# Where the image statistics of a sample are taken: from the local to the global attention's turns, and two group norms on ScalarE

## The chip, the core and the metric

The kernel runs on one core of a Trainium2 chip. The metric is the time of one execution on the device, in microseconds (us). A core has TensorE (PE in the profile; its weight loads are PEld), VectorE (DVE), ScalarE (ACT), GpSimd (POOL) and SyncE (SP), which here only issues transfers. Each engine works through its own list of instructions in order, and waits where an instruction needs the result of another engine.

## What is computed

Four layers follow one another on four samples of 56 x 56 x 128 values. Each takes a group norm of its input and adds its result to it:

```python
x = x + _L0_conv_ref(_gn(x), ...)   # window attention, global attention, MLP
x = x + _L1_conv_ref(_gn(x), ...)   # edge layer
x = x + _L2_conv_ref(_gn(x), ...)   # spectral attention over the channels' images
x = x + _L3_conv_ref(_gn(x), ...)   # convolution
```

Layer 2 normalizes every image (one channel of one sample, 56 x 56) by its own mean and variance, of the values that its group norm gives. These are the image statistics of which this document speaks.

## The kernel before, in words

The samples are taken one after the other through layers 0 and 1 (`first_layers`, called for b = 0 to 3), with the channels in the 128 partitions. For each sample:

1. **Local attention** (`fast_windows`, L307). The 3136 tokens lie in 8 groups of 392. A loop over n sets the order by hand: in step n group n+2 is normed (`norm`, L366, through the helper at L193, on DVE), group n is projected (`project`, L371 to L379: TensorE, then the heads' queries w_qd by turns on DVE, L225, and ScalarE, L223), group n-1 is scored, and so on for the later stages. Norms 0, 1 and 2 stand ahead of project(0) on DVE. Three sets of buffers w_xg, w_kT, w_qd, w_vd, w_pT are set to zero by POOL at the start (L339 to L345), w_qd fourth. The order of TensorE, ScalarE and DVE is the order of the program; POOL's memsets are placed by the scheduler.
2. **Global attention** (`fast_layer`, L615). The queries lie in 7 blocks of 448 and the keys in 24 chunks of 128, for four heads. One unit is one head's scores of one chunk. A turn (L840) makes 7 units: `scores(0)` of four units into PSUM banks 0 to 3, `scores(1)` of three into banks 4 to 6 (L818), one exponential for each (L821) into a ring of 28 slots (7 chunks), then some `values` matmuls (L684). The first 28 units are made beside the rest of the local attention's projections; the turns after that are counted here from 1, and there are 92. A bank holds 512 values for each partition, a score uses 448. The softmax's denominators need the sum over the chunks: DVE adds the chunks (`f_acc`, L669 and L673), 5 of the 24 are added by transfers (`f_far`: the first on SP, L661, four on POOL, L663), and DVE adds f_far last but one (L672). After a block `finish` takes f_acc through TensorE (L715 to L721), and DVE inverts the result (L728). The remainder of the keys is scored at L704, and from block 3 on an earlier block is centred at L743. At the end a square root's table is loaded (L862).
3. MLP, then the **edge layer** (`e_` tiles), whose result x1 goes to memory (x2d, L2812).

**The image statistics** of sample b-1 are taken beside sample b's layer 0. `normed_images` (L1480) is a generator: each `yield` ends a step. Its steps are 28 pairs of `bn_stats` on the 56 rows of x1 (L1492), their aggregate (L1496), a small matmul (L1499) that averages over the channels of a group, three small operations, a second small matmul (L1508), the copy of its result s_var and six small operations, a square root on ScalarE (L1523), four operations for mean and scale, a third matmul (L1532, s_mean) and its copy to `norm`, a fourth (L1541, s_sq) and its copy to s_d, four instructions that norm x1 in place (L193 on x), after the last of them two transfers on SP (xat L1548, xad L1550), and a last root (L1552) with two operations. `yield "root"` stands ahead of each of the two roots.

In the kernel before, `fast_windows` takes one such step after every stage of the local attention (`run` and `step`), a matmul's result goes into a bank of the rotation that the stages use (`bank`), and the two roots are put right behind the local attention's own roots (`root`, L445), for which the table is loaded anyhow. Sample 0 has no sample ahead of it, so there are no steps in its local attention. The last sample's statistics are taken later, in layer 2, and are not concerned.

Of the kernel before, what the change touches and what calls it, by code (L numbers as in the profile page):

```python
# [12 lines left out]
F32 = mybir.dt.float32  # L13
AF = mybir.ActivationFunctionType
ALU = mybir.AluOpType
# [4 lines left out]
P = 128  # L20
B = 4
HH = 56
TOK = HH * HH
NB = 448
# [167 lines left out]
def apply_norm(k, out, xt, mr):  # L192
    k.nc.vector.tensor_scalar(out, xt, mr[:, 0:1], mr[:, 1:2], ALU.subtract, ALU.mult)  # L193
# [110 lines left out]
    mlp(k, w, xf, xw, x1, st)  # L304


def fast_windows(k, w, xw, xf, mr, beside, Q, K, V, h1, inverse):  # L307

# [6 lines left out]
    nc, tc = k.nc, k.tc  # L317
# [3 lines left out]
    N = 8 * WIN  # L321
# [4 lines left out]
    with ExitStack() as es:  # L326
# [6 lines left out]
        for i in range(BUFS):  # L333
            xg = big.tile([P, N + 16], F32, name="w_xg%d" % i)
            kT = big.tile([P, N + 16], F32, name="w_kT%d" % i)
            qd = big.tile([P, 8, 4, WIN], F32, name="w_qd%d" % i)
            vd = big.tile([P, 4, 4, 2, 33], F32, name="w_vd%d" % i)
            pT = big.tile([P, 16 * WIN + 16], F32, name="w_pT%d" % i)
            nc.gpsimd.memset(xg[:, N:], 0.0)  # L339
            nc.gpsimd.memset(kT[:, N:], 0.0)  # L340
            nc.gpsimd.memset(pT[:, 16 * WIN:], 1.0)
            nc.gpsimd.memset(qd, 0.0)
            nc.gpsimd.memset(vd, 0.0)
            for par in range(2):
                nc.gpsimd.memset(vd[halves[par], :, :, par, 32], 1.0)  # L345
            fixed.append((xg, kT, qd, vd, pT))
# [16 lines left out]
            return slice(g * N, (g + 1) * N)  # L363

        def norm(g):
            apply_norm(k, fixed[g % BUFS][0][:, :N], xw[:, g * N:(g + 1) * N], mr)  # L366

        def project(g):
            xg, kT, qd, vd, pT = fixed[g % BUFS]
# [73 lines left out]

        def root(i):
            nc.scalar.activation(inverse[:, i, :], roots[i][:, :N], AF.Sqrt, scale=1024.0, bias=eps)  # L445
            step(True)

        def invert(i):
            nc.vector.reciprocal(inverse[:, i, :], inverse[:, i, :])
# [25 lines left out]
                nc.vector.tensor_copy(V[:, chunk:chunk + m, :].rearrange("p a c -> p (a c)"), pm[:, :m * P])  # L475
                chunk += m

        steps = beside(bank)
        root_next = False

        def step(root):
            nonlocal root_next
            if root or not root_next:
                root_next = next(steps, None) == "root"

        def run(*stages):
            for stage, g in stages:
                if 0 <= g < NG:
                    stage(g)
                    step(False)  # L490

        norm(0)
        norm(1)
        for n in range(NG + 1):
            run((norm, n + 2), (project, n), (score, n - 1), (value, n - 2), (turn, n - 3), (output, n - 4),
                (central, n - 5), (variance, n - 6))
        variance(3)
        root(0)
# [2 lines left out]
        invert(0)  # L501
        run((turn, 7), (output, 6), (central, 5), (output, 7), (central, 6), (variance, 4), (variance, 5))
        run((divide, 0), (central, 7), (attended, 0), (variance, 6), (divide, 1), (variance, 7))
        while not root_next and next(steps, "end") not in ("root", "end"):
            pass
        root(1)
        nc.scalar.activation(eps, k.eps, AF.Exp)
        run((attended, 1))
        invert(1)
        for _ in steps:  # L510
            pass
    rest = [((divide, 2),)] + [((attended, g), (divide, g + 1)) for g in range(2, 7)] + [((attended, 7),)]

    def finish(n):
# [97 lines left out]
LAST_ONES = (22, 23)  # L612


def fast_layer(k, w, xw, xf, x1, st, beside, mr):  # L615

# [6 lines left out]
    with ExitStack() as es:  # L625
# [3 lines left out]
        va = big.tile([P, 25, P], F32, name="f_va")  # L629
        oT = big.tile([P, TOK], F32, name="f_oT")  # L630
        inverse = big.tile([P, 2, 8 * WIN], F32, name="f_inverse")
        use = fast_windows(k, w, xw, xf, mr, beside, qT, kT, va, oT, inverse)

        ring = es.enter_context(tc.tile_pool(name="f_ring", bufs=1)).tile([P, RING, NB], F32, name="f_ring")
        wk = es.enter_context(tc.tile_pool(name="f_wk", bufs=2))
# [111 lines left out]
        def deviation(i0, m, n):  # L747
            for q in range(m):
                nc.tensor.matmul(pm[32 * q:32 * q + 32, n, :NB], k.ones_c[:, 0:32], qT[:, blk(i0 + q)],
                                 start=True, stop=True)  # L750
            r = kT[:32 * m, blk(i0)]
            nc.scalar.activation(r, pm[:32 * m, n, :NB], AF.Sqrt, scale=1024.0, bias=eps[:32 * m])
            nc.vector.reciprocal(r, r)
# [54 lines left out]
        with tc.manual_schedule(engines={mybir.EngineType.PE, mybir.EngineType.Activation, mybir.EngineType.DVE}):  # L808
            t, special, n_bank = 0, 0, 0

            def scores(n):
                nonlocal t
                m = (4, 3)[n]
                ss = bank(n)
                for i in range(m):
                    j, c = divmod((t + i) // 4, 24)
                    h = (t + i) % 4
                    nc.tensor.matmul(ss[:, i, :NB], kT[heads[h], c * P:(c + 1) * P], qT[heads[h], blk(j)],  # L818
                                     start=True, stop=True)
                slot = t % RING  # L820
                nc.scalar.activation(ring[:, slot:slot + m, :], ss[:, :m, :NB], AF.Exp, scale=scale)  # L821
                for q in range(t // 4, (t + m) // 4):
                    queue.append((*divmod(q, 24), WHOLE))
                    add(*divmod(q, 24))
                t += m

            def other_banks():
                nonlocal n_bank
                n_bank += 1
                return pm[:, 4 + n_bank % 3, :]  # L830

            windows_rest, n_rest = use(other_banks)
            for n in range(n_rest):
                scores(0)
                values(2)
                windows_rest(n)
                ready.extend(queue)
                queue.clear()
            turn = 0
            while t < 96 * NBLK:  # L840
                scores(0)
                scores(1)
                values(ROOM[turn % 4] + (len(ready) > 3))
                turn += 1
                ready.extend(queue)
                queue.clear()
                if special < NBLK and t >= 96 * special + 7 and (not special or hasattr(blocks[special - 1], "raw")):
                    j = special
                    special += 1
                    remainder(j)  # L850
                    if j >= 3:
                        centre(j - 3, 6)
                    if not j:
                        ready.append((0, 24, WHOLE))
                    else:
                        started = hasattr(blocks[j], "po")
                        finish(j - 1, j if started else None)
                        if not started:
                            ready.append((j, 24, WHOLE))

            last = NBLK - 1
            nc.scalar.activation(root, k.eps, AF.Sqrt)  # L862
            deviation(0, 4, 3)
            while ready:
                values(4)
            copied = finish(last)
            divide(0, 4, 4)
            copied()
            centre(4, 2)
            hidden(0)  # L870
            hidden(1)
            result(0)
            nc.tensor.matmul(pm[:, 5, :NB], w.wo, oT[:, blk(last)], start=True, stop=True)
            output(last, pm[:, 5, :NB])
            centre(5, 6)
            hidden(2)
            centre(6, 7)
            result(1)
            deviation(4, 3, 5)
            hidden(3)  # L880
            result(2)
            divide(4, 3, 5)
            for wi in range(3, 8):
                if wi < 7:
                    hidden(wi + 1)
                result(wi)
            statistics(7)
# [592 lines left out]
def normed_images(k, w, st, b, wk, bank, xp, xad, xat):  # L1480
# [48 lines left out]
    yield  # L1529
    nc.vector.tensor_scalar(sq, sq, mr[:, 1:2], mr[:, 1:2], ALU.mult, ALU.mult)  # L1530
    ps = bank()
    nc.tensor.matmul(ps[:, 64:64 + HH], k.ones_c, mean, start=True, stop=True)  # L1532
    yield
    nc.vector.tensor_copy(st.norm[:, b, 0, :], ps[:, 64:64 + HH])
    nc.vector.tensor_sub(d, mean, st.norm[:, b, 0, :])
    yield
    nc.vector.tensor_mul(d, d, d)
    nc.vector.scalar_tensor_tensor(sq, d, float(HH), sq, ALU.mult, ALU.add)
    yield
    ps = bank()  # L1540
    nc.tensor.matmul(ps[:, 128:128 + HH], k.ones_px, sq, start=True, stop=True)  # L1541
    yield
    nc.vector.tensor_copy(d, ps[:, 128:128 + HH])
    yield
    for t in range(0, HH, 14):
        apply_norm(k, x[:, t:t + 14, :], x[:, t:t + 14, :], mr)
# [1205 lines left out]
def build(k, packs, I, out):  # L2752
# [3 lines left out]
    with ExitStack() as es:  # L2756
# [16 lines left out]
        with tc.tile_pool(name="w01", bufs=1) as wp, tc.tile_pool(name="io", bufs=1) as io:  # L2773
            xw = io.tile([P, TOK], F32, name="xw")
            with ExitStack() as pre:
# [24 lines left out]

                input_norms(k, x, wp, wk, psum, between())
                small_scores = scores_are_small(k, bounds, wp, wk)

            def first_layers(front, x, to, loaded=False):
                if not loaded:
                    nc.sync.dma_start(xw, x)
                xf = io.tile([P, TOK], F32, name="xf")
                st = io.tile([P, 9, 6], F32, name="x1_st")
                front(k, w0, xw, xf, x1, st)
                edge_layer(k, w1, x1, st)  # L2810
                if to is not None:
                    nc.sync.dma_start(to, x1)  # L2812
# [6 lines left out]

            with tc.If(small_scores > 0) as small:  # L2820
                for b in range(B):
                    first_layers(lambda *a: fast_layer(*a, functools.partial(norms, b - 1), k.mr[:, b, :]), I["x"][b],
                                 x2d[b] if b < B - 1 else None, loaded=b == 0)
            with small.Else():
                with tc.For_i(0, B, 1) as b:
# [78 lines left out]
```

## Time and profile before

| | us |
|---|---|
| median of 3 runs (lowest, highest) | 3538.7 (3538.6, 3540.94) |
| the profiled execution | 3539.16 |
| its span, from first to last instruction | 3537.4 |
| TensorE busy in the span | 3314.4 (94%) |
| DVE, ScalarE, POOL busy | 2706.5, 2101.2, 1252.5 |
| local attention of samples 0, 1, 2, 3: from ScalarE's first w_qd to the first exponential of the global attention | 67.6, 79.5, 79.4, 78.7 |
| global attention of samples 0 and 1: from there to the root after it (L862) | 365.0, 365.0 |

The profile is one execution. Its page shows each engine's busy time, the chain of instructions that ended last (75% of it on TensorE, 15% on DVE) and the costliest groups of instructions. A timeline lists instructions of one stretch: start, duration, engine, line, operation, output and inputs, how many were merged (x2; the duration is then that of the stretch), and in brackets the idle time of the engine before it with what ended it. A matmul in float32 is recorded as two. The table "by windows" gives each engine's busy time in a stretch, its number of instructions in brackets, the clock that TensorE was granted (1.00 is full) and what the transfers moved.

### The profile page before, as it was taken

How to read it: one execution, taken by the hardware profiler on the slowest of the kernel's cores; microseconds unless marked ns; L12 is line 12 of the kernel's file. 1: busy time of each engine (PE TensorE's matmuls, PEld its weight loads, DVE VectorE, ACT ScalarE, POOL GpSimd, SP SyncE). 2: the span in 40 equal slices, each digit the busy share in tenths (PEclk: the TensorE clock that was granted, in tenths of full speed). 3: DMA queues.
4: the chain of work that ended last, by engine and by line, in shares of the span. 5: the costliest groups of instructions: out<-in, count | busy, mean ns of one | idle time of the engine just before them, and what ended most of it. 6: DMA issues, size and time to landing. Idle time of an engine off the chain costs nothing.

```text
span 3537.4 us, 64240 instructions
## 1 busy us (share of the span) xinstructions
PE 3314.4 (94%) x27710; PEld 1425.1 (40%) x27710; DVE 2706.5 (77%) x2566; ACT 2101.2 (59%) x2199; POOL 1252.5 (35%) x764
## 2 busy tenths in 40 slices
PE   6999998889999898999999889999888899999998
PEld 4433333353333434333343443333337443336664
DVE  6588868867888597688859858887795778886776
ACT  4688866558888564788857558887553012214442
POOL 1000007600000491000019400000673778884686
PEclk8999999999999999999999999999998999999999
DMA  2143420014343000444310024442003037753101
GB/s 104 43 93 86 96 52 19 19 48 95 87 92 84 19 1 20 100 95 95 89 45 1 19 61 95 92 98 60 37 14 99 6 70 175 183 139 92 55 19 55
DMA packets 98011, 243.40 MB, mean 69 GB/s; under 512 B 64456, under 2 KB 69832, under 8 KB 92712
## 3 DMA queue, kind: packets, MB, share of 16 engines
q0 software_dynamic: 16128, 102.77, 14.4%
q1 hardware_dynamic: 74872, 123.61, 12.0%
q10 hardware_dynamic: 6720, 12.85, 1.3%
q8 instruction: 219, 3.59, 0.4%
q14 instruction: 72, 0.59, 0.1%
HBM read 79.43 MB, written 31.33 MB: 31 GB/s over the span
## 4 chain that ended last, share of the span: by engine, by line
PE 75%; DVE 15%; ACT 4%; issue 3%; POOL 2%; DMA 0%; DVEq 0%; POOLq 0%; ACTq 0%
PE f_pm L818 18%; PE f_pm L684 15%; PE u_po L1941 8%; DVE e_td L1222 7%; PE e_acc L1277 3%; PE q_acc L1795 3%; PE f_pm L791 2%; PE f_pm L770 2%; PE e_pa L1190 2%; ACT f_ring L821 1%; PE f_pm L464 1%; PE o_d L2204 1%; DVE f_acc L673 1%; PE o_d L2601 1%; PE f_pm L715 1%
## 5 line engine op out<-in xcount | busy, mean ns | idle before, releaser
L821 ACT ACTIVATE f_ring<-f_pm 128x1792 f32<-128x1792 f32 (+1 forms) x764 | 1093.8, 1482 | 229.3 <-PE f_pm L818 181.6
L673 DVE TENSOR_TENSOR f_acc<-f_acc,f_ring 128x1792 f32<-128x1792 f32 x468 | 947.6, 2025 | 191.3 <-ACT f_ring L821 160.2
L818 PE MATMUL f_pm<-f_qT,f_kT 32*128 32x448 f32 x5376 | 725.4, 571 | 15.7 <-ACT f_ring L821 5.1
L684 PE MATMUL f_pm<-f_ring,f_va 128*32 128x448 f32 (+1 forms) x6304 | 589.8, 490 | 0.0
L663 POOL DMA_DIRECT2D f_far<-f_ring x112 | 96.6, 862 | 1333.3 <-ACT f_ring L821 1062.6
L1222 DVE TENSOR_TENSOR e_td<-e_a,e_pc 128x1792 f32<-128x1792 f32 (+1 forms) x288 | 493.1, 1778 | 15.1 <-ACT e_c L1210 15.0
L1224 POOL TENSOR_TENSOR e_tp<-e_a,e_c 128x1792 f32<-128x1792 f32 (+1 forms) x152 | 453.6, 3021 | 74.4 <-issue 42.5
L818 PEld LDWEIGHTS f_pm<-f_qT,f_kT 32*128 32x128 f32 x5376 | 260.0, 183 | 418.0 <-ACT f_ring L821 304.6
L684 PEld LDWEIGHTS f_pm<-f_ring,f_va 128*32 128x32 f32 x6304 | 163.8, 109 | 410.1 <-issue 397.8
L1936 DVE TENSOR_TENSOR u_ud<-u_px,u_d 112x1792 f32<-112x1792 f32 x144 | 263.5, 1863 | 39.6 <-PE u_po L1941 35.4
L1277 PE MATMUL e_acc<-e_td,t_edge 128*32 128x448 f32 x2016 | 225.4, 543 | 42.5 <-DVE e_td L1222 42.3
L1226 ACT ACTIVATE e_tp<-e_tp 128x1792 f32<-128x1792 f32 (+1 forms) x152 | 236.9, 1583 | 44.9 <-POOL e_tp L1224 44.4
L1938 POOL TENSOR_TENSOR u_up<-xh,u_d 112x1792 f32<-112x1792 f32 (+1 forms) x72 | 240.8, 3372 | 55.1 <-PE u_po L1941 41.3
L1941 PE MATMUL u_po<-u_ud,AT 112*64 112x448 f32 x1056 | 213.7, 544 | 1.9 <-DVE u_ud L1936 1.9
L1277 PE MATMUL e_acc<-e_tp,t_edge 128*32 128x448 f32 x1120 | 131.1, 540 | 3.3 <-ACT e_tp L1226 3.3
L1277 PEld LDWEIGHTS e_acc<-e_td,t_edge 128*32 128x32 f32 x2016 | 55.5, 109 | 191.1 <-DVE e_td L1222 116.0
L1941 PEld LDWEIGHTS u_po<-u_ud,AT 112*64 112x64 f32 x1056 | 74.3, 138 | 128.8 <-issue 112.9
L728 DVE RECIPROCAL f_den<-f_den 128x448 f32<-128x448 f32 x28 | 82.6, 2951 | 44.9 <-ACT f_den L725 44.9
L1780 POOL TENSOR_TENSOR q_u<-iS,q_g 128x1792 f32<-128x1792 f32 x32 | 102.8, 3235 | 23.0 <-PE q_acc L1795 23.0
L1795 PE MATMUL q_acc<-q_u,S 64*64 64x448 f32 x1024 | 104.6, 553 | 4.4 <-DVE q_u L1782 3.3
L1941 PE MATMUL u_po<-u_up,AT 112*64 112x448 f32 x480 | 103.9, 546 | 2.4 <-POOL u_up L1938 2.4
L1190 PE MATMUL e_pa<-e_xg,t_edge 128*128 128x448 f32 x224 | 101.0, 577 | 5.1 <-DVE e_xg L193 5.1
(526 smaller groups left out, 4435.6 us busy)
## 6 DMA issues: line engine op xcount, KB each, us to landing
f_far<-f_ring POOLq DMA_DIRECT2D x112, 896.0 KB, 6.3
u_d<-dd SPq DMA_DIRECT2D x46, 784.0 KB
f_far<-f_ring SPq DMA_DIRECT2D x28, 896.0 KB
xw<-in_x SPq DMA_DIRECT2D x4, 1568.0 KB
x2d<-x SPq DMA_DIRECT2D x4, 1568.0 KB
xat<-x SPq DMA_DIRECT2D x4, 1568.0 KB
x_xs<-xat ACTq DMA_DIRECT2D x32, 196.0 KB
xm<-x_ev ACTq DMA_DIRECT2D x64, 98.0 KB
```

What stands on the lines that cost most here:

```text
L673: nc.vector.tensor_add(e.acc, e.acc, slots(j, c))
L684: nc.tensor.matmul(e.po[heads[h], part], va[o, c, heads[h]], p, start=(c == 0), stop=(c == 23 and part.stop == NB))
L818: nc.tensor.matmul(ss[:, i, :NB], kT[heads[h], c * P:(c + 1) * P], qT[heads[h], blk(j)], start=True, stop=True)
L821: nc.scalar.activation(ring[:, slot:slot + m, :], ss[:, :m, :NB], AF.Exp, scale=scale)
L1222: nc.vector.tensor_tensor(t, am, cm, ALU.max)
L1224: nc.gpsimd.tensor_sub(t, am, cm)
L1226: nc.scalar.activation(tf, tf, AF.Relu)
L1277: nc.tensor.matmul(acc[quarters[r0 + r], :NB], w.S[:, 0, :], t[:, r].rearrange("p l n -> p (l n)"), start=(g == 0), stop=False)
L1795: nc.tensor.matmul(acc[bp][i][halves[hb % 2], hb // 2, :NB], x[o], u[o, 8 * hb:8 * hb + 8, :].rearrange("p h t -> p (h t)"), start=first, ...
L1936: nc.vector.tensor_mul(u, bc(px[:, :, :NB], 2, m), dm)
L1938: nc.gpsimd.tensor_mul(u, bc(x, 2, m), dm)
L1941: nc.tensor.matmul(po[64 * b2:64 * b2 + 64, :NB], st.AT[:, 8 * i + h0 + q, 2 * bp + b2, :], u[:, b2, q, :], start=(left == 16), stop=(left ...
```

## The change

- `normed_images` is no longer handed to `fast_windows`. `fast_layer` makes the generator (`steps`) and takes one step at the end of each turn of the global attention, from the third turn on, until the second `"root"`; what is left (the last root and two operations) is issued behind the turns, after the table for the square root is loaded. The first root now falls into the turns, between exponentials, so that the built program loads ScalarE's table twice there.
- The results of its four small matmuls go into the 64 values of bank 3 that the scores leave unused (`pm[:, 3, NB:]`).
- Norms 0 and 1 of the local attention are done by ScalarE, as x times scale plus a shift, which is made once for all samples. Norms 2 and on stay on DVE; in step 0 project(0) goes ahead of norm(2). In the built order DVE has norm 2 and norm 3 one after the other, behind project(0) and ahead of project(1).
- POOL's memset of w_qd comes second, not fourth.
- In the built order the local attention of samples 1 to 3 has, from project(0) on, the instructions of sample 0.

```diff
         def norm(g):
-            apply_norm(k, fixed[g % BUFS][0][:, :N], xw[:, g * N:(g + 1) * N], mr)
+            out, x = fixed[g % BUFS][0][:, :N], xw[:, g * N:(g + 1) * N]
+            if g < 2:
+                nc.scalar.activation(out, x, AF.Identity, bias=shift, scale=mr[:, 1:2])
+            else:
+                apply_norm(k, out, x, mr)
...
         def root(i):
             nc.scalar.activation(inverse[:, i, :], roots[i][:, :N], AF.Sqrt, scale=1024.0, bias=eps)
-            step(True)
...
-        steps = beside(bank)
-        root_next = False
-
-        def step(root):
-            nonlocal root_next
-            if root or not root_next:
-                root_next = next(steps, None) == "root"
-
         def run(*stages):
             for stage, g in stages:
                 if 0 <= g < NG:
                     stage(g)
-                    step(False)
...
         for n in range(NG + 1):
-            run((norm, n + 2), (project, n), (score, n - 1), (value, n - 2), (turn, n - 3), (output, n - 4),
+            begin = [(norm, n + 2), (project, n)]
+            run(*(begin if n else begin[::-1]), (score, n - 1), (value, n - 2), (turn, n - 3), (output, n - 4),
                 (central, n - 5), (variance, n - 6))
...
+            steps, rooted = beside(lambda: pm[:, 3, NB:]), 0
             windows_rest, n_rest = use(other_banks)
...
                 scores(1)
                 values(ROOM[turn % 4] + (len(ready) > 3))
                 turn += 1
+                if turn > 2 and rooted < 2:
+                    rooted += next(steps, None) == "root"
                 ready.extend(queue)
...
             nc.scalar.activation(root, k.eps, AF.Sqrt)
+            for _ in steps:
+                pass
             deviation(0, 4, 3)
...
-    nc.tensor.matmul(ps[:, 64:64 + HH], k.ones_c, mean, start=True, stop=True)
+    nc.tensor.matmul(ps[:, 2:2 + HH], k.ones_c, mean, start=True, stop=True)
...
+                k.shift = wp.tile([P, B], F32, name="shift0")
+                nc.vector.scalar_tensor_tensor(k.shift, k.mr[:, :, 0], -1.0, k.mr[:, :, 1], ALU.mult, ALU.mult)
```

## The prediction

> **What bounds the kernel now.** I first read the windows of the sample parts. Sample 0's local attention has no image statistics beside it, sample 1's has. The windows run from ScalarE's first w_qd to the first exponential of the global attention; the third is sample 0's global attention.
>
> ```profile
> core 0: us, PE busy (x) PEld busy (x) DVE busy (x) ACT busy (x) POOL busy (x), PEclk, DMA share, GB/s
> 55.30:122.86 67.56, 65.69 (x650) 43.05 (x646) 38.80 (x80) 43.62 (x76) 3.86 (x12) 0.98 0.01 1
> 695.40:774.86 79.46, 70.48 (x659) 44.14 (x658) 51.37 (x157) 44.16 (x77) 1.95 (x8) 0.95 0.18 41
> 122.86:487.88 365.02, 360.38 (x3242) 123.00 (x3244) 294.90 (x161) 298.98 (x232) 24.26 (x28) 1.00 0.40 89
> ```
>
> See two things. The statistics cost the local attention 79.46 - 67.56 = 11.9 us, although DVE is only 65% busy. The global attention is bound by TensorE: 360.4 of 365.0 us. There DVE (295) and ScalarE (299) have room on average, but each microsecond for which TensorE itself waits is lost.
>
> The timeline of sample 1 (start, duration, then the idle before it) shows how the statistics cost it:
>
> ```profile
> 754.42 0.82 PE L427 MATMUL w_mm<-w_oT,t_first 128*128 128x392 f32 x2
> 758.55 0.67 PE L1541 MATMUL w_late<-s_sq,c_ones_px 128*128 128x56 f32 x2 [3.30 <-DVE s_sq L1538]
> 759.01 1.63 PE L432 MATMUL w_mm<-xf,c_centre 128*128 128x392 f32 x2
> ```
>
> A matmul of 56 columns stood in TensorE's order until DVE, behind a 2.60 us reciprocal (L449), had its input; everything behind it waited 3.30 us, and then ran at half speed (window 760 to 765: clock 0.52). So the small chain hurts by waits in TensorE's order, not by its 20 us of DVE work.
>
> The start of sample 1's local attention:
>
> ```profile
> 689.16 3.70 DVE L193 TENSOR_SCALAR w_xg<-xw,mr 128x392 f32<-128x392 f32 x1
> ...
> 688.77 1.41 POOL L342 MEMSET w_qd<- 128x1568 f32 x1
> ...
> 695.40 0.58 ACT L223 ACTIVATE w_qd<-w_mm,t_first 32x392 f32<-32x392 f32 x1 [10.53 <-DVE w_qd L225]
> ```
>
> The first norm takes 3.70 us beside POOL's memsets, where the median of this row is 0.47.
>
> **Pages.** The Trainium skill, "SBUF — State Buffer", section "SBUF: two separate sides", says that a GpSimd instruction and a two-port Vector instruction lock each other out of a shared port pair for whole instructions, and that ScalarE's ports wait for nobody. The 3.70 against 0.47 us agrees; for the moved norms I go by L223's 0.58. "TensorE: Matmul & The Clock Gate", section "What's actually happening", has the clock halve after about one idle window of 3.4 us. The trace had it after 3.30 us idle in all three samples, but not after the waits of 1.33 us in the edge layer (clock 1.00); I go by the trace and take 3 us as the doubtful edge.
>
> **The change, part by part** (per sample 1 to 3 unless said).
>
> (a) Statistics leave the local attention. Its duration becomes sample 0's, which has exactly that order: 79.46, 79.40 and 78.73 become 67.56. Gain 11.9 + 11.8 + 11.2 = **34.9**.
>
> (b) Norms 0 and 1 on ScalarE, w_qd's memset first. ScalarE idled 10.53 us there. Norm at 688.65 + 0.6, two projections of 0.8, and DVE's first w_qd at 690.3 instead of 694.69; the memset (1.41 us from 688.67) is done at 690.1. But norms 2 and 3 stay on DVE, now ahead of project(1), and POOL's memsets run until 697.4: each waits for the end of a memset, about 694.4 and 696.2. Project(1)'s w_qd then comes at 696.3 instead of 698.97: **2.7**; bounds 1.0 (one memset more) and 4.3 (no lock). For sample 0, 0.5 by the same count. Sum 8.6. One shift of 0.15 us on DVE: nothing, beside the branch.
>
> (c) 28 pairs of statistics (0.33 us each) in the turns of the global attention, one a turn. A turn lasts 3.35 us; DVE's adds are 2.03 (pitch 2.1). At the ends of blocks 0 and 1 DVE finished f_acc at 844.93 and 893.83, TensorE took it at 846.41 and 895.35: 1.5 us in hand; three or four pairs fall behind the last idle, 1.0 to 1.3 us. Cost 0. Block 2's end lies behind the stall of (g): 0. At block 3's end four x norms (0.62) meet 1.7 us in hand: 0.3.
>
> (d) Four small matmuls in TensorE's order: 0.3 each, as 753.00 to 753.26: 1.2.
>
> (e) Their waits. The changed build's order shows each at the end of a turn, right after a turn whose DVE step makes its input. Beside the s_mv matmul (turn 32, TensorE ready at 919.7), DVE still has two adds to 919.9 and then the aggregate of 1.67: wait 2.0. For s_mean (turn 41, ready 954.5), DVE has the reciprocal of f_den and two adds to 956.2, then three small ones: 2.3. For s_t and s_sq three turns of adds lie between: 0. Sum 4.3.
>
> (f) The new banks' release. The small matmul's result stands in the unused columns of bank 3, and the changed order shows that two turns after each small matmul the fourth score matmul of the turn, the one that writes bank 3, waits for DVE: for the copy of that result. The copy is queued behind the adds of its own turn, which need that turn's exponentials. Here is such a turn:
>
> ```profile
> 929.26 1.78 PE L818 MATMUL f_pm<-f_qT,f_kT 32*128 32x448 f32 x14
> ...
> 930.36 2.85 ACT L821 ACTIVATE f_ring<-f_pm 128x1792 f32<-128x1792 f32 x2 [0.51 <-PE f_pm L818]
> ...
> 930.97 1.71 PE L684 MATMUL f_pm<-f_ring,f_va 128*32 128x448 f32 x16
> 932.61 1.78 PE L818 MATMUL f_pm<-f_qT,f_kT 32*128 32x448 f32 x14
> ...
> 928.71 10.54 DVE L673 TENSOR_TENSOR f_acc<-f_acc,f_ring 128x1792 f32<-128x1792 f32 x5 [1.22 <-ACT f_ring L821]
> ```
>
> From a turn's start: exponentials end at 2.7 and 3.95, an add takes 2.1, and TensorE wants bank 3 at 3.35 + 0.75 = 4.1. Counted with each turn's chunks: copy of s_mr behind one add on the first exponential, 4.95 + delay of the aggregate: wait 1.25. Copy of s_var behind three adds, the last on the second exponential: 7.0, wait 3.0. Copy of norm behind two adds: 7.5, wait 3.4. Copy of s_d behind an add delayed by the two before it: 5.9, wait 1.85. Sum **9.5**. Behind TensorE wait ScalarE's exponentials, and POOL's far adds behind those. No row shows this wait; bounds 0 (if DVE were always in time) and 13 (each behind two late adds).
>
> (g) Square root of the variance in turn 38: two table loads and a root on ScalarE. Row L862 gives 1.28 a load and its neighbours touch it; root 0.28: 2.84, of which 0.4 was idle. TensorE's next use of those banks (L704, L743) comes **2.15** later. The last root (0.33) and DVE's 0.7 at the end come before f_kT, which is needed 1.4 us after it is made: 0.
>
> (h) The idles of (f), about 2.7 and 3.1 us, touch the clock's edge; half speed cost 1.5 to 3 us in the local attention. I take 1.
>
> (i) SP: xat and xad leave the gap between stages (762 to 775) and go ahead of block 4's first f_far. Their issue holds SP 7.7 us and they move 3.2 MB in 13 us. A ring slot comes round in 15 us and its transfer needs 7.2. I take 0; at worst 5 us, when the transfers share the time.
>
> **Sum.** Gains 34.9 + 8.6 = 43.5. Costs per sample 0.3 + 1.2 + 4.3 + 9.5 + 2.15 + 1 = 18.45, times 3 = 55.4. Net +11.9. The profiled run took 3539.2 us (span 3537.4 and 1.8 around it), 0.5 above the median of 3538.7, which is within the runs' spread. 3539.2 + 11.9 = **3551**.
>
> **Rivals.**
> *Faster: bank 3 comes free in time.* One mechanism: if the copies are taken before TensorE returns to bank 3, (f) and with it (h) fall: 3539.2 - 43.5 + 3 x 7.95 = 3519.6. For it: DVE waits for ScalarE at most adds (160 us over 161), so it is often on time. Against it: the copy stands behind adds on its own turn's exponentials, and 4.8 is later than 4.1 even without delay. It decides when the four waits sum to under 6.5 us a sample.
> *About the same.* The waits overlap with ScalarE's lag and come to 5 to 8 us: 3533 to 3545.
> *The clock gate and the transfers.* Both long idles halve the clock (2 x 2.3 in place of 1) and xat makes ScalarE wait 2 us for ring slots: +3 x 5.6: 3568.
> *The norms gain nothing* because DVE waits for POOL's last memset: 8.6 down to 3: 3557; inside the first case.
>
> **Numbers.** First case (3545 to 3561) 0.5, gate and transfers 0.18, about the same 0.17, faster 0.15. Likeliest 3551; its own range is 3545 to 3561. Differences under 0.2% (7 us) can't be told from none here: slower 0.68, same 0.17, faster 0.15. Range 3527 to 3567: it cuts off most of the faster case and the worst of the slow one.
>
> **What would show it.** (a) first w_qd to first exponential in samples 1 to 3 near 67.6. (b) DVE's norms 2 and 3 long, project(1)'s w_qd some 7.6 us after POOL's first memset. (e), (f) TensorE idle before the s_mv and s_mean matmuls and before four L818 rows a sample, released by DVE. (g) two loads of 1.28 beside a TensorE idle of 2. (h) a clock under 1 near turns 36 and 43. The global attention at about 382 us in samples 1 to 3, 365 in sample 0. It is wrong if those attentions stay under 379.

## The result and the profile after

The change makes the kernel slower by 0.65%: 3563.9 us (3557.7 to 3564.9, six runs) against 3540.3 (3538.6 to 3542.0, six runs); ratio 1.0065, 95% interval 1.0053 to 1.0078. The forecast was 3551, 3527 to 3567, slower with 0.68. The direction and the range held; the time is 13 us above the likeliest value, and above that case's own range by 3.

The page of the kernel after, first its span, then its first part (busy time), then TensorE's row of score matmuls; the fourth line is that row in the kernel before:

```profile
span 3563.1 us, 64248 instructions
...
PE 3330.2 (93%) x27710; PEld 1432.2 (40%) x27710; DVE 2687.9 (75%) x2559; ACT 2114.9 (59%) x2213; POOL 1252.2 (35%) x764
...
L809 PE MATMUL f_pm<-f_qT,f_kT 32*128 32x448 f32 x5376 | 734.2, 576 | 34.5 <-DVE s_var L1507 8.0
...
L818 PE MATMUL f_pm<-f_qT,f_kT 32*128 32x448 f32 x5376 | 725.4, 571 | 15.7 <-ACT f_ring L821 5.1
```

The span grew by 25.7 us. TensorE has the same number of instructions; it is busy 16 us longer and idle 10 us longer. Ahead of the score matmuls it is idle 34.5 us instead of 15.7, and the largest part, 8.0, was ended by VectorE's s_var, a result of the moved statistics. The windows tell where, in this order: the local attention of sample 1, and the global attention of samples 0 and 1.

```profile
core 0: us, PE busy (x) PEld busy (x) DVE busy (x) ACT busy (x) POOL busy (x), PEclk, DMA share, GB/s
694.86:763.29 68.43, 64.27 (x650) 42.17 (x648) 40.42 (x81) 43.75 (x75) 6.17 (x19) 1.00 0.05 19
124.83:491.50 366.67, 362.03 (x3242) 123.62 (x3244) 294.89 (x161) 299.04 (x231) 24.28 (x28) 1.00 0.40 89
763.29:1152.64 389.35, 372.12 (x3250) 126.23 (x3252) 306.73 (x240) 301.71 (x234) 24.12 (x28) 0.97 0.41 92
```

The local attention gained what was forecast (79.46 became 68.43, at full clock). The global attention of sample 1 paid more: 389.35 us, not 382, with 10 us more of busy TensorE than in sample 0, at a mean clock of 0.97. Its matmuls are the same ones plus four small ones, so most of that busy time is matmuls at half speed.

The timeline of TensorE in sample 1, only the rows that waited over a microsecond in the two blocks (of seven) in which the small matmuls fall; the same two blocks of the kernel before have no such row:

```profile
911.70 0.35 PE L1495 MATMUL f_pm<-s_mv,t_shared 128*128 128x1 f32 x2 [1.64 <-DVE s_mv L1492]
...
927.23 1.88 PE L809 MATMUL f_pm<-f_qT,f_kT 32*128 32x448 f32 x8 [2.64 <-DVE s_var L1507]
...
944.33 0.98 PE L695 MATMUL f_pm<-f_qT,f_kT 32*64 32x448 f32 x8 [1.90 <-ACT f_ring L812]
...
959.19 0.40 PE L1528 MATMUL f_pm<-s_mean,c_ones_c 128*128 128x56 f32 x2 [2.24 <-DVE s_mean L1524]
...
966.65 1.13 PE L809 MATMUL f_pm<-f_qT,f_kT 32*128 32x448 f32 x8 [1.49 <-DVE norm L1530]
...
980.18 1.03 PE L809 MATMUL f_pm<-f_qT,f_kT 32*128 32x448 f32 x8 [1.61 <-DVE s_d L1539]
```

All forecast waits are there but the one for s_mr: L1495 and L1528 are (e), L809 released by VectorE is (f), L695 behind the table loads is (g). Each is shorter than forecast. The windows show what was missed. They are laid on a grid of 3.41 us; read TensorE's busy time in one row and the clock in the next:

```profile
909.43:912.84 3.41, 1.77 (x19) 0.81 (x13) 3.41 (x3) 1.16 (x1) 0.86 (x1) 1.00 0.18 36
912.84:916.26 3.42, 3.42 (x22) 0.94 (x19) 2.04 (x2) 2.85 (x2) 0.00 (x0) 0.50 1.00 201
916.26:919.67 3.41, 3.38 (x38) 1.25 (x30) 1.02 (x4) 1.60 (x2) 0.00 (x0) 1.00 0.18 36
923.08:926.49 3.41, 1.51 (x14) 0.31 (x6) 3.31 (x2) 1.02 (x1) 0.00 (x0) 1.00 1.00 202
926.49:929.90 3.41, 2.67 (x16) 0.83 (x20) 0.85 (x3) 0.72 (x1) 0.00 (x0) 0.50 0.17 34
929.90:933.32 3.42, 3.42 (x24) 1.03 (x19) 2.34 (x2) 2.13 (x2) 0.00 (x0) 0.50 0.00 0
940.15:943.56 3.41, 2.29 (x22) 0.42 (x16) 1.83 (x1) 3.37 (x4) 0.00 (x0) 1.00 0.02 5
943.56:946.97 3.41, 2.44 (x18) 0.66 (x18) 1.48 (x1) 3.41 (x5) 0.00 (x0) 1.00 0.49 202
```

A window with 1.64 us idle is followed by one at exactly half clock, 3.41 us long. The wait of 1.90 us ahead of L695 straddles two windows (1.12 and 0.97 idle), and the clock stays full. So short waits, which the prediction took for harmless below 3 us, can slow the matmuls behind them: 5, 5 and 3 such windows in these two blocks of samples 1, 2 and 3, where the kernel before had none.

**Where the 25.7 us are.** The profiled execution is cut at GpSimd's first memset of a sample, at the first exponential of the global attention, at the reciprocals of f_den that close each block, and at the next sample's memset. From memset to first exponential: 46.2 us gained over four samples. From there to the first reciprocal: 4.8 lost. From the first to the seventh: 22.0, 21.6 and 20.1 lost in samples 1 to 3 and none in sample 0. The rest of the samples: 0.7 lost. Ahead of sample 0: 2.7 lost. Sum 25.7.

### The profile page after: what moved, and what is told of

Read it like the earlier page. It is cut to its first block, busy times and chain, and to the rows that moved or that the text cites. A ratio compares the mean times of both kernels' runs of the same rounds, so it can differ in the third digit from the quotient of the medians.

```text
span 3563.1 us, 64248 instructions
## 1 busy us (share of the span) xinstructions
PE 3330.2 (93%) x27710; PEld 1432.2 (40%) x27710; DVE 2687.9 (75%) x2559; ACT 2114.9 (59%) x2213; POOL 1252.2 (35%) x764
## 3 DMA queue, kind: packets, MB, share of 16 engines
q1 hardware_dynamic: 74872, 123.61, 11.9%
## 4 chain that ended last, share of the span: by engine, by line
PE 74%; DVE 15%; ACT 5%; issue 4%; POOL 2%; DMA 0%; DVEq 0%; POOLq 0%; ACTq 0%
PE f_pm L809 16%; PE f_pm L675 14%; PE u_po L1937 8%; DVE e_td L1218 6%; PE e_acc L1273 3%; DVE f_acc L664 3%; PE q_acc L1791 3%; ACT f_ring L812 3%; PE e_pa L1186 2%; PE f_pm L782 2%; PE f_pm L761 2%; PE w_ss L394 1%; PE f_pm L467 1%; PE o_d L2200 1%; PE f_pm L706 1%
## 5 line engine op out<-in xcount | busy, mean ns | idle before, releaser
L809 PE MATMUL f_pm<-f_qT,f_kT 32*128 32x448 f32 x5376 | 734.2, 576 | 34.5 <-DVE s_var L1507 8.0
L675 PE MATMUL f_pm<-f_ring,f_va 128*32 128x448 f32 (+1 forms) x6304 | 601.8, 499 | 0.0
L809 PEld LDWEIGHTS f_pm<-f_qT,f_kT 32*128 32x128 f32 x5376 | 261.9, 184 | 436.9 <-ACT f_ring L812 295.3
```

What stands on the lines that cost most here:

```text
L675: nc.tensor.matmul(e.po[heads[h], part], va[o, c, heads[h]], p, start=(c == 0), stop=(c == 23 and part.stop == NB))
```

## The experiments

Each run is told with its ratio to the kernel before on the same chip. That kernel's median there was 3540 to 3543, its single runs 3535 to 3551, so the stretches of the traces decide more than the medians. Here blocks are counted from one, by the reciprocal that closes them (the prediction counts from zero: its block 4 is block 5 here). The small matmuls fall into blocks 3 and 4, from the second to the fourth reciprocal: 99.96 us before and 122.41 after in sample 1.

**1. The norms alone**, on the kernel before:

```diff
+            if g < 2:
+                nc.scalar.activation(out, x, AF.Identity, bias=shift, scale=mr[:, 1:2])
...
+            run(*(begin if n else begin[::-1]), (score, n - 1), ...
```

> The kernel before with the norm part alone: norms 0 and 1 of the local attention on ScalarE, w_qd's memset first, the projection of group 0 ahead of norm 2; the image statistics stay in the local attention. From the two traces this part is worth about 3.5 us in each of samples 1 to 3 and 0.7 in sample 0, 11.2 in all: 3540.3 - 11.2 = 3529 (3526 to 3533). By the prediction's own term (b) it is 8.6: 3531.7. Rival, that the norms gain nothing because VectorE waits for GpSimd's memsets instead: 3540 or more.

Measured: 3535.5, ratio 0.9981 (0.9974 to 0.9987). A gain, but 6.8 us and not 11. From memset to first exponential, sample 1 took 86.24 us where the kernel before took 86.23: the s_mv matmul came 1.5 us earlier, and one more window at half clock took it back ahead of s_mean. Sample 2 likewise; sample 3 gained 3.8 us. While the statistics stand in the local attention, their waits take most of what the norms bring; the two parts don't add up.

**2. The statistics alone**, on the kernel after:

```diff
-            if g < 2:
-                nc.scalar.activation(out, x, AF.Identity, bias=shift, scale=mr[:, 1:2])
-            else:
-                apply_norm(k, out, x, mr)
+            apply_norm(k, out, x, mr)
...
-            run(*(begin if n else begin[::-1]), (score, n - 1), ...
+            run(*begin, (score, n - 1), ...
```

> The kernel after with the norm part undone (norms, memsets and projection of the kernel before): only the statistics have moved. If the two parts add up: 3563.9 + 11.2 = 3575 (3570 to 3580), the local attention of samples 1 to 3 at 67.6 us from the first w_qd to the first exponential. Rival, that the late start of the local attention is what shifts the global attention into its bad waits: at or under 3564.

Measured: 3572.7, ratio 1.0085 (1.0072 to 1.0099). With the statistics gone the norms are worth 8.8 us by the medians (7 if each kernel is compared with the kernel before on its own chip), beside the 8.6 of (b). From memset to first exponential samples 1 to 3 took 74.6, 74.0 and 73.5: that is 35.9 us for (a), and 10.3 more in the kernel after, with sample 0, for (b). The start does not shift the later waits: blocks 3 and 4 took 121.2 to 123.5 us, and 120.9 to 122.6 after.

**3. The waits filled**, on the kernel after: six score matmuls repeated ahead of each wait, which write what the scores write.

```diff
+                    if i == 3 and n == 0 and turn == fill_at:
+                        again(2)
...
+            def again(n):
+                for i in range(3 * n):
+                    ...
+                    nc.tensor.matmul(pm[:, i % 3, :NB], kT[heads[h], c * P:(c + 1) * P], qT[heads[h], blk(j)],
...
+                if now:
+                    again(2)
```

> The kernel after with six repeated score matmuls (1.5 us) put where TensorE waits for VectorE: ahead of the s_mv and s_mean matmuls, and ahead of the score matmul that waits for the copies of s_var, norm and s_d. They write what the scores write anyway, so nothing else changes; the waits stay, but TensorE is not idle in them. Theory: the waits cost twice, once as idle time (12.6 us a sample) and again because an idle of about 1.5 us in one 3.41 us window halves TensorE's clock for the next window (8.5, 8.5 and 5.1 us in samples 1 to 3). Filled, the second part goes: 3563.9 - 20 = about 3544 (3540 to 3551), no half-clock spells near these waits. Rival, that idle time alone is the cost and the slow matmuls are waiting for data: 3560 to 3575, with the spells still there.

Measured: 3561.1, ratio 1.0059 (1.0046 to 1.0073). My theory failed here. The half-clock windows in blocks 3 and 4 fell from 13 to 5 over three samples, as planned, and the time hardly moved: from the first to the seventh reciprocal, 961.4 us over three samples, and 963.5 after. The timeline of this run, sample 1, shows why:

```profile
907.26 0.38 PE L1514 MATMUL f_pm<-s_mv,t_shared 128*128 128x1 f32 x2
...
912.52 1.03 PE L811 MATMUL f_pm<-f_qT,f_kT 32*128 32x448 f32 x8 [0.94 <-DVE s_mr L1518]
...
915.35 0.38 PE L1523 MATMUL f_pm<-s_t,t_shared 128*128 128x1 f32 x2 [0.53 <-ACT f_ring L814]
...
922.79 1.03 PE L811 MATMUL f_pm<-f_qT,f_kT 32*128 32x448 f32 x8 [1.13 <-DVE s_var L1526]
```

From the s_mv matmul to the next small one it is 8.09 us; in the kernel after, with a half-clock window between them, 8.08. At full clock TensorE only runs earlier into the wait for VectorE's copy of s_mr (0.94, the wait that "was missing" after) and for ScalarE (0.53). Here, where a wait on VectorE comes next, the half-clock window ahead of it cost nothing. Idle time and slow matmuls can't be added as if each could be had back by itself.

**4. No waits**: ScalarE copies each small result in the turn of its matmul, and three of the small matmuls come a turn later.

```diff
     nc.vector.bn_aggr(mv, rows.rearrange("p a b -> p (a b)"))
     yield
+    yield
...
     nc.tensor.matmul(ps[:, 0:1], k.g4, mv[:, 0:1], start=True, stop=True)
-    yield
     mr = wk.tile([P, 2], F32, name="s_mr", bufs=1)
+    nc.scalar.copy(mr[:, 0:1], ps[:, 0:1])
+    yield
...
-    nc.vector.tensor_copy(mr[:, 0:1], ps[:, 0:1])
```

> The kernel after with the waits taken away: each small matmul's result is copied by ScalarE in the same turn (not by VectorE a turn later), and the s_mv, s_t and s_mean matmuls come one turn later than before. The same statistics, the same adds, the same table loads and transfers. Theory (waits and the clock they cost): idle goes from 12.6 to about 3 us a sample (the table loads' 1.9 and the small matmuls' 1.2 stay), the half-clock spells go: 3563.9 - 3 x 9.5 - 20 = about 3515 (3507 to 3523), faster than both kernels. Rival, that the load is what costs (20 us more on VectorE and the transfers in a stage with little room): 3545 or more.

Measured: 3532.3, ratio 0.9975 (0.9967 to 0.9983): faster than both kernels, but 17 us short. Blocks 3 and 4 took 104.0 us in sample 1, with none of the waits. What is missing is in block 5, 58.0 us against 51.3, in each of the three samples (20 us in all). The timeline of this run there (SPq is SP's queue):

```profile
987.83 7.31 SPq L1548 DMA_DIRECT2D xad<-x  x1
995.25 0.47 SPq L652 DMA_DIRECT2D f_far<-f_ring  x1
...
1004.72 2.85 ACT L812 ACTIVATE f_ring<-f_pm 128x1792 f32<-128x1792 f32 x2 [6.38 <-DMA f_far<-f_ring]
...
1006.44 1.13 PE L809 MATMUL f_pm<-f_qT,f_kT 32*128 32x448 f32 x4 [4.24 <-ACT f_ring L812]
```

The transfers of the x norms stand ahead of the block's far transfer in SP's order, and in this run they come two steps of the generator later, which is 11 us nearer to the block's end. So the far transfer leaves 3.5 us behind the fourth reciprocal, where without them it leaves 7.5 us ahead of it. ScalarE waits 6.38 us for the ring slot that it reads, TensorE 4.24, and two windows at half clock follow. This is the worst case of (i). The kernel after escapes it: its far transfer leaves 6.4 us ahead of that reciprocal, 1.1 late, and block 5 takes 51.3 as before.

**5. The copies alone**: run 4 without the later turns; the cut is against run 4.

```diff
     nc.vector.bn_aggr(mv, rows.rearrange("p a b -> p (a b)"))
     yield
-    yield
     ps = bank()
...
```

> The kernel after with the four small results copied by ScalarE in the turn of their matmul instead of by VectorE a turn later; nothing else is moved, so the waits of the s_mv and s_mean matmuls stay, and the transfers leave in the same turn as in the kernel after. It asks what the release of bank 3 alone costs, term (f). If those waits are the larger half: blocks 3 and 4 of samples 1 to 3 go from 122.4 us to about 108 (104 without any wait, and 1.6 + 2.2 of waits): 3563.9 - 3 x 14 = 3522 (3516 to 3530). Rival, that all these waits are one chain paced by VectorE's adds, so that removing some makes the others longer: 115 us and more, 3542 or more.

Measured: 3533.3, ratio 0.9972 (0.9961 to 0.9984). Between the two expectations: blocks 3 and 4 took 111.7, 111.1 and 110.0 us. The waits for the copies are gone and the others did not grow (1.64, 1.91 and 2.23 in sample 1, and within 0.01 in the others), so it is not one chain. The release of bank 3, with the half-clock windows that it brings, is worth 33.2 us over three samples (first to seventh reciprocal), 11.1 each: (f) is the largest cost.

**6. The transfers later**, on run 4:

```diff
+    for _ in range(12):
+        yield
     for t in range(0, HH, 14):
         apply_norm(k, x[:, t:t + 14, :], x[:, t:t + 14, :], mr)
```

> The kernel without waits (the run before this one) with the x norms and the two transfers behind them 12 turns later, in the middle of a block and not just ahead of a block's first far transfer on SP. There ScalarE waited 6.38 us for that far transfer, TensorE 4.24, and the clock fell for two windows; block 5 took 58.0 us against 51.3. If the transfers are the cause, block 5 returns to 51.3 in samples 1 to 3: 3532.3 - 3 x 6.8 = 3512 (3506 to 3518). Rival, that they only move the wait to the next block's far additions: 3525 or more.

Measured: 3508.4 (3495.7 to 3511.8), ratio 0.9899 (0.9885 to 0.9913): 1.0% faster than the kernel before, the fastest version. Block 5 is 51.3 again in samples 1 to 3. The transfers did not land in the middle of a block, but ahead of the next far transfer; that one leaves 2.2 us late, and nobody waits for it. The windows of this run, global attention of sample 1, with all of the statistics in it:

```profile
759.09:1128.37 369.28, 362.58 (x3250) 124.49 (x3252) 305.94 (x236) 302.14 (x239) 24.15 (x28) 1.00 0.43 97
```

VectorE is as busy as in the kernel after (305.9 against 306.7) and the stage takes 369 us instead of 389, at full clock. So the load of the statistics on VectorE was not what cost the 20 us.

**7. No table loads**, on run 6: the root by nine Newton steps on VectorE.

```diff
-    nc.scalar.activation(t1, var, AF.Sqrt, bias=k.eps)
+    for i in range(9):
+        nc.vector.reciprocal(inv, t1)
+        nc.vector.scalar_tensor_tensor(t1, inv, var, t1, ALU.mult, ALU.add)
+        nc.vector.tensor_scalar_mul(t1, t1, 0.5)
...
```

> The same, with the square root of the variance in the turns made by VectorE: nine Newton steps of three 1-column instructions over five turns, so no table load and no root on ScalarE in the attention. Term (g): the two loads made TensorE wait 1.9 us a sample. If that is its cost: 3 x 1.9 = 5.7 us under the run with later transfers, 3506 where that gives 3512. Rival, that 28 more instructions on VectorE make its adds late: no gain, or up to 3 us slower.

Measured: 3521.8, ratio 0.9948 (0.9934 to 0.9961), slower than run 6. Only 5 us of the 13 lie in the global attention (TensorE waits 1.91 us for s_mean again); most of the rest, 8.6 us, lies behind it in the last sample's stretch. `normed_images` also makes the last sample's statistics, in layer 2, so the Newton steps run there too: from that sample's aggregate (s_mv) to the end of its last x norm it is 55.1 us, where run 6 took 47.1, and the spectral attention behind it starts 7.8 us later. The run doesn't test (g): in run 6 the loads lie in another turn, and block 3 is 50.4 us with and without them.

**8. The first root left out**, on run 5 (the image statistics are then not the reference's), to measure (g) where it lay:

```diff
-    nc.scalar.activation(t1, var, AF.Sqrt, bias=k.eps)
     yield
     yield
-    nc.vector.reciprocal(mr[:, 1:2], t1)
+    nc.vector.reciprocal(mr[:, 1:2], var)
```

> The run with the copies on ScalarE, and the first square root left out (the reciprocal is taken of the variance itself, so the image statistics are not the reference's): no table load in the turns. It measures term (g) where it lies. There TensorE waited 1.91 us for ScalarE ahead of block 3's remainder. If (g) costs what it shows: blocks 3 and 4 together 1.9 us shorter a sample, more where a half-clock window behind it goes too (up to 3.6). Rival, that the loads stand beside a wait that comes anyway: less than 1 us.

Its result stands with that of run 9.

**9. The two waits of (e) filled**, on run 5, by the matmuls of run 3:

```diff
+            fills = [2, 0, 2, 0]
+
+            def small_bank():
+                for i in range(3 * fills.pop(0)):
+                    ...
+                return pm[:, 3, NB:]
...
-            steps, rooted = beside(lambda: pm[:, 3, NB:]), 0
+            steps, rooted = beside(small_bank), 0
```

> The run with the copies on ScalarE, with six repeated score matmuls (1.7 us) ahead of the s_mv and the s_mean matmul, so that TensorE is busy in these two waits and resumes when it did. No copy of VectorE's follows that it would have to wait for. Question: does a half-clock window cost its 1.7 us here, where it cost nothing ahead of a wait? If it does: no such windows behind s_mv and s_mean, and s_mv to the remainder's matmuls 1.3 us shorter than in the run without the filling (27.1 us) where that had a window. If half-clock windows are always hidden by what follows: the same times as before.

Measured: single runs of 3526.4 (run 8) and 3521.9 (run 9), beside one of 3543.3 for the kernel before. Run 9 has no half-clock window in blocks 3 and 4 of any sample: 108.5, 108.5 and 108.9 us, where run 5 has 2, 2 and 1 windows and 111.7, 111.1 and 110.0. From the s_mv matmul to the remainder's (L695) in sample 1, the windows of run 5 and then of run 9:

```profile
911.81:938.91 27.10, 24.95 (x214) 8.58 (x214) 20.77 (x17) 21.83 (x19) 1.20 (x2) 0.94 0.34 69
```

```profile
907.66:933.27 25.61, 23.51 (x218) 8.42 (x215) 20.76 (x17) 21.84 (x19) 1.08 (x2) 1.00 0.36 73
```

The half-clock window costs 1.5 us here, where no copy on VectorE follows to hide it. Run 5 had no such window at this place in sample 3 and took 25.73 there. Run 8 in sample 1, where it had no window either, has block 3 at 51.49 against run 9's 53.79: the table loads cost 2.3 us in this sample. Block 4 doesn't change (54.81 and 54.75).

## Why the prediction was right, and what it mis-sized

Sums in us over samples 1 to 3 (with sample 0 for (a) and (b)):

| step | forecast | measured | by |
|---|---|---|---|
| (a) statistics leave the local attention | -34.9 | -35.9 | before to run 2 |
| (b) norms and memset | -8.6 | -10.3 | run 2 to after |
| (c), (d) pairs, four small matmuls | 4.5 | 10.2 | what run 6 keeps |
| (e) waits for s_mv, s_mean | 12.9 | 7 | run 8 to run 6, sample 1: 1.13 and 1.20 |
| (f) release of bank 3 | 28.5 | 33.2, with its clock windows | after to run 5 |
| (g) table loads | 6.5 | 6.9 | run 9 to run 8, sample 1 |
| (h) clock, apart from (f)'s | 3.0, with (f)'s | 6.8 | run 5 to run 9 |
| (i) transfers | 0 | 0; 20 in run 4 | run 4 to run 6 |
| start of the global attention, preamble, rest | 0 | 8.2 | traces |

The forecast's terms sum to 11.9. The measured ones sum to 26.1, against the 25.7 of the spans; (e) and (g) stand for three samples by one. The sizes of (e) to (h) hold for the order in which the runs took these parts away: the copies first, then the clock, the loads and the last waits. Run 3 took most of the half-clock windows away first and got 2 us.

**(a), (b)** held. At the start of sample 1 ScalarE has its two norms done in 1.32 us, and VectorE's norms 2 and 3 wait for GpSimd's memsets as forecast; the timeline:

```profile
692.37 1.32 ACT L368 ACTIVATE w_xg<-xw,shift,mr 128x392 f32<-128x392 f32 x2 [3.69 <-PE e_po L1231]
692.45 0.12 POOL L339 MEMSET w_xg<- 128x16 f32 x1 [13.28 <-PE e_po L1231]
...
696.85 2.83 DVE L193 TENSOR_SCALAR w_xg<-xw,mr 128x392 f32<-128x392 f32 x2
...
699.59 0.61 DVE L225 TENSOR_SCALAR w_qd<-w_mm,t_first 32x392 f32<-32x392 f32 x1
```

Project(1)'s w_qd comes 7.14 us behind the first memset (forecast 7.6, before 10.3). Two norms of 0.47 us took 2.83 beside the memsets, which agrees once more with what the Trainium skill says of the shared ports ("SBUF — State Buffer", section "SBUF: two separate sides").

**(f)** was the right mechanism and decides the direction: without its 33.2 us the measured terms sum to a gain. Its visible waits (s_var 2.64, norm 1.49, s_d 1.61 in sample 1, none for s_mr) sum to 5.7 us and not 9.5, in part because TensorE at half clock arrives later (at full clock, in run 3, it did wait for s_mr, 0.94 us); with the clock the cost is 11.1 a sample. The rival that bank 3 comes free in time decided from "under 6.5 us a sample". By the waits alone it would have seemed right; the removal shows that it was not.

**(h)** is the step that failed: "I take 3 us as the doubtful edge". The clock fell after waits of 1.5 us, and (e) and (g) too brought half-clock windows, not only the two long idles of (f): 6.8 us from run 5 to run 9, beside those that are counted in (f). The profile of the kernel before had already shown it, in two windows at the start of sample 3's global attention: TensorE is idle once in the first, for 1.29 us, and the second is at half clock.

```profile
2078.90:2082.31 3.41, 2.12 (x21) 0.57 (x17) 2.40 (x4) 1.95 (x2) 0.00 (x0) 1.00 0.41 170
2082.31:2085.72 3.41, 3.41 (x12) 1.51 (x5) 0.00 (x0) 1.97 (x2) 0.00 (x0) 0.50 0.26 107
```

The edge of 3 us rested on two kinds of wait alone, 3.30 and 1.33 us. The rival with clock gate and transfers (3568) comes nearest in value, but half of its mechanism, the transfers, did not happen.

**(e)** was too large by 2 us a sample. The waits had the forecast length (1.64 and 2.24 against 2.0 and 2.3), but taking them away brought only 1.2 us each: TensorE then waited 0.47 and 0.82 us for ScalarE.

**(c), (d)** were too small: 3.4 us a sample remain in run 6, whose turns are not quite those of the kernel after. The two waits for ScalarE are 1.3 of them and four small matmuls about 1.3; the last microsecond stays open.

**Not in the sum**: 4.8 us between first exponential and first reciprocal, most of it one half-clock window in each of samples 0 and 1 (sample 3 has one before and after), and 2.7 in the preamble, ahead of sample 0. These vary without the change: in the nine kernels of the experiments the preamble took 49.8 to 53.0 us, and the stretch to the first reciprocal took 74.4 us without such a window and 76.1 with one in sample 0, where the code of that stretch is the same. The forecast had no term for it, and it came on the slow side, as far as these runs show by chance: without it the measured terms sum to 17.9 us, against the forecast's 11.9. So the direction does not hang on it, but more than half of the forecast's shortfall does. Six executions of the kernel after differ by 7 us.

## What to carry to other kernels

When small work is put into the turns of a stage that TensorE bounds, put every result where its reader's engine is done first: here a copy by ScalarE in the same turn instead of by VectorE behind the next turn's adds turned 0.65% slower into 0.3% faster, and with three small matmuls and one queue's transfers in later turns it became 1.0%. Beside the idle time of a wait on TensorE look at the clock of the next window, and ask what comes next: here a half-clock window cost 1.5 us where TensorE then had free way, and nothing ahead of a wait that another engine ended. To price a wait, take it away in a run; the bracket in the timeline is neither its lower nor its upper bound: 1.64 and 2.24 us of (e) brought 1.2 each, and 5.7 of (f) brought 11.1.

## What the hardware showed

TensorE's clock followed a fixed grid of 3.41 us windows in every trace, whatever stage began when. Counted over blocks 3 to 5 of samples 1 to 3 in all eleven traces, windows at full clock: with less than 1.45 us idle, none of 1422 was followed by one at half clock; with 1.45 to 2.0 us, 31 of 45; with more than 2.0, all 12. Over the whole of these traces it is less sharp: 47 of 310 with 1.0 to 1.45 us idle, 58 of 138 with 1.45 to 2.0, 134 of 170 with 2.0 to 3.4. So the idle time of a window does not decide alone. In run 5 the same wait of 1.64 us ahead of the s_mv matmul fell whole into one window, in sample 1 (first pair) and in sample 3 (second pair), and only the first was followed by half clock:

```profile
909.52:912.93 3.41, 1.77 (x18) 0.97 (x13) 3.41 (x3) 1.34 (x3) 0.86 (x1) 1.00 0.18 36
912.93:916.35 3.42, 3.42 (x23) 0.95 (x19) 1.43 (x2) 2.52 (x2) 0.00 (x0) 0.50 1.00 201
2210.00:2213.41 3.41, 1.77 (x21) 0.61 (x13) 3.41 (x3) 2.04 (x2) 0.86 (x1) 1.00 0.34 67
2213.41:2216.82 3.41, 3.37 (x35) 1.55 (x38) 1.79 (x2) 2.25 (x3) 0.00 (x0) 1.00 1.01 202
```

What else decides is not shown. The Trainium skill, "TensorE: Matmul & The Clock Gate", section "What's actually happening", says that the window is free-running and 3413 ns long, which the traces agree with; it gives one idle window as the condition for the fall, and here less than half a window was enough (1.49 of 3.41 us), so the trace decides. Where a wait falls on the grid differs between samples and executions, and the same code then takes some 1.5 us more or less (27.06 to 27.10 us against 25.73 in run 5).
